# A gated recurrence on one core: the second half of each step's scans worked chunk by chunk

## The chip, the cores and the metric

The kernel runs on one core of a Trainium2 chip. A core has a matrix engine (TensorE, PE in the profile; its weight loads are shown as PEld), a vector engine (VectorE, DVE), a scalar engine for activation functions (ScalarE, ACT), a general engine (GpSimd, POOL) and a queue engine for transfers (SyncE, SP). The metric is the device time of one execution in microseconds (us). The median of three runs before the change is 1750.26 us (1750.22 to 1751.6).

## The reference

Cut to what is computed (all float32; batch 8, 512 time steps, 512 inputs and 512 state values):

```python
def step(h, x_t):
    fused = sigmoid(concatenate([x_t, h], -1) @ w_W + w_b)
    hidden_state, output_state = split(fused, 2, axis=-1)            # r, z
    memory_state = x_t @ wx_W + wx_b + hidden_state * (h @ wh_W + wh_b)
    h_new = output_state * h + (1.0 - output_state) * tanh(memory_state)
    return h_new, h_new
out = x + hs                # hs: h_new of all 512 steps
```

In the kernel's words a step is: `r` and `z` from sigmoids, `hh = h @ wh_W + wh_b`, `xx = x_t @ wx_W + wx_b`, the memory `m = r * hh + xx`, `n = tanh(m)`, and `h_new = z * h + (1 - z) * n`. The next step can't start its products before it has `h_new`.

## The kernel before

**Layout.** The 512 state values lie as four chunks of 128 on the partitions, with the batch (8) along the free dimension. Half A is chunks 0 and 1, half B is chunks 2 and 3. A group is four steps (`GS`); the step's place in its group is `s`, and `rows = slice(8 * s, 8 * s + 8)`.

**TensorE.** In each of the 512 steps (`for i in range(T)`, L208) the state is the stationary operand, 32 columns of `hT` for one chunk, and the weights `wh` stream past it. Four column groups `j` are done side by side (L221). The string `ORDER` (L25) sets the order by hand: R0 R1 G0 G1 R2 R3 G2 G3 H0 H1 H2 H3. The letter names the PSUM bank, the digit the chunk. So R<-hTA and G<-hTA (chunks 0 and 1) come first, then R<-hTB and G<-hTB (chunks 2 and 3), then H<-hTA and H<-hTB, and at the end of the step one part of the prefill `xp`, the input product for the group after the next (L223). Bank R holds the sums for `r` of both halves, G those for `hh` and `z` of half A, H those for `z` and `hh` of half B. A bank can be read once all four chunks have been added.

**From the banks to the next state.** The order of VectorE's work is written out at L294 to L303: both `turn_r`, then for half A `turn_h`, `turn_z`, `memory`, `update`, and the same four for half B. `turn_r` and `turn_z` transpose 128x64 values from PSUM to SBUF (L237), and ScalarE turns them into `r` in slot 1 of `md0` and `1 - z` in slot 2 of `hd0` (through the helper `act`, L157). `turn_h` transposes `hh` into slot 0 of `md1` (L255). `memory` runs a scan along the free dimension (L273): out = d0 * previous + d1, over pairs of slots, where a zero in slot 0 of `md0` restarts the recurrence and leaves `hh`, and slot 1 makes `r * hh + xx`. ScalarE's tanh of it goes to slot 1 of the state tile `hT`. `update` is a scan over triples of slots (L285): d0 is `hd0` with 0, -1, 1 - z in its slots, d1 is `hT` with h, n, h in its slots, so that slot 2 of the next `hT` is `(n - h) * (1 - z) + h`. ScalarE then copies the new state from slot 2 into slot 0 (L305), for the next update.

**Tiles.** `hT`, `md0`, `md1` and `hd0` of either half have the shape partition, row, chunk, slot (L109 to L116). The two chunks of a half thus alternate row by row: of one chunk, neighbouring rows of `md1` lie 16 bytes apart and those of `hT` 24.

**Around it.** After the updates, VectorE transposes a part of `xx` for the next group (`turn_x`, L187), ScalarE copies a part of the prefill into the next group's banks (`spread`, L182) or the bias into `xp` (`seed`, L165), VectorE sets `IDLE` = 5 small cells of a tile that nothing reads (L314), and POOL adds `x` to the new state into the output tile `ot`, half B first (L316). SP loads an input chunk and stores an output chunk every 16 steps. Where two instructions write and read across engines, a semaphore wait is put between them from the regions they touch. The call to `manual_schedule` (L205) leaves the order of the loop as written.

Of the kernel before, what the change touches and what calls it, by code (L numbers as in the profile page):

```python
# [7 lines left out]
F32 = mybir.dt.float32  # L8
AF = mybir.ActivationFunctionType
ALU = mybir.AluOpType  # L10
PSUM = bass.MemoryType.PSUM

P = 128
NQ = 4
GS = 4
B = 8
# [2 lines left out]


DVE_FILL = 15
IDLE = 5
SYNC = mybir.DependencyInfo(mybir.DependencyClass.Sync, mybir.DependencyReason.DATA)

ORDER = "R0 R1 G0 G1 R2 R3 G2 G3 H0 H1 H2 H3"  # L25
# [7 lines left out]
def tile_cond_rnn_residual(  # L33
# [7 lines left out]
    out: bass.AP,  # L41
    TC: int,
):

# [20 lines left out]
    nc = tc.nc  # L67
# [4 lines left out]
    const = ctx.enter_context(tc.tile_pool(name="const", bufs=1))  # L72
    xin_p = ctx.enter_context(tc.tile_pool(name="xin", bufs=4))
    out_p = ctx.enter_context(tc.tile_pool(name="outp", bufs=3))
    work = ctx.enter_context(tc.tile_pool(name="work", bufs=4))
# [4 lines left out]
    def load_x(c):  # L80
        if c < NCH:
            t_ = xin_p.tile([P, NQ, TC * B], F32, tag="xin", name=f"xin_{c}")
            nc.sync.dma_start(out=t_, in_=x[c].rearrange("p (k n) -> p k n", k=NQ))
            xins[c] = t_
# [16 lines left out]
    for k in range(NQ):  # L101
        nc.sync.dma_start(out=wh[:, k], in_=wh_d[:, k])
    load_x(1)
    load_x(2)

    NH = 2 * GS
    hT = [  # L109
        [const.tile([P, 32, 2, 3], F32, name=f"hT{n}{i}") for i in range(NH)]  # L110
        for n in "AB"
    ]

    md0 = [[const.tile([P, 32, 2, 2], F32, name=f"md0{n}{i}") for i in range(2)] for n in "AB"]
    md1 = [[const.tile([P, 32, 2, 2], F32, name=f"md1{n}{i}") for i in range(2)] for n in "AB"]
    hd0 = [[const.tile([P, B, 2, 3], F32, name=f"hd0{n}{i}") for i in range(2)] for n in "AB"]  # L116
    zeros = const.tile([P, 512], F32, name="zeros")
    nc.vector.memset(zeros, 0.0)
    for n, t_ in enumerate(hd0[0] + hd0[1] + md0[0] + md0[1] + hT[0] + hT[1]):
# [1 line left out]
    for t_ in hd0[0] + hd0[1]:  # L121
        nc.gpsimd.memset(t_[:, :, :, 1], -1.0)
    idle = const.tile([P, IDLE], F32, name="idle")

    def state(hf, i, slot=2):

        s = i % GS
        return hT[hf][i % NH][:, B * s : B * s + B, :, slot]
# [13 lines left out]
    def mm(out_, lhsT, rhs, start=False):  # L142
        nc.tensor.matmul(  # L143
            out_, lhsT, rhs, start=start, stop=False, skip_group_check=True
        )
# [10 lines left out]
    def act(key, out_, in_, func, **kw):  # L156
        inst = nc.scalar.activation(out_, in_, func, **kw).ins  # L157
        if key in written:
            tc.declare_no_dep(inst, written[key], reason="ordered through VectorE")
        written[key] = inst  # L160
        return inst

    def seed(g):

        nc.scalar.copy(xps[g % 2], bias)  # L165

    def prefill(g):

        c, t0 = divmod(g * GS, TC)
        for k in range(NQ):  # L170
            for j in range(NQ):
                mm(
                    xps[g % 2][32 * j : 32 * j + 32, 64:448],
                    xins[c][:, k, t0 * B : t0 * B + 32],
                    wx[:, k, j, :],
                )
            yield

    def spread(g, names):

        for n in names:
            nc.scalar.copy(banks[g % 2][n], xps[g % 2][:, XP[n]])  # L182

    def turn_x(g, e):

        c0 = XP["X"].start + 32 * e
        nc.vector.transpose(  # L187
            md1[e // 2][g % 2][:, :, e % 2, 1], xps[g % 2][:, c0 : c0 + 32]
        )

    def take(it, n=None):
        while n is None or n > 0:
            if next(it, it) is it:
                return
            n = None if n is None else n - 1
# [12 lines left out]
    for i in range(T):  # L208
        g, s = divmod(i, GS)
        c, t = divmod(i, TC)  # L210
        ps = banks[g % 2]
        if t == 0:
            load_x(c + 3)
            ot = out_p.tile([P, NQ, TC, B], F32, tag="ot", name=f"ot_{c}")
        if s == 0:
            pre = prefill(g + 2) if g + 2 < NG else iter(())

        for n in ORDER.split():
            bank, k = n[0], int(n[1])
            hs = hT[k // 2][i % NH][:, :, k % 2, 2]  # L220
            for j in range(NQ):  # L221
                mm(ps[bank][32 * j : 32 * j + 32, :], hs, wh[:, k, j, WH[bank]])
        take(pre, 1)  # L223

        rows = slice(B * s, B * s + B)
        def flat(t_):
            return t_.rearrange("p n c s -> p (n c s)")

        raw = {
            "h": (ps["G"][:, :HU], ps["H"][:, HU:]),  # L230
            "z": (ps["G"][:, HU:], ps["H"][:, :HU]),
            "r": (ps["R"][:, :HU], ps["R"][:, HU:]),
        }

        def turned(n, hf):
            t_ = work.tile([P, 2, 32], F32, tag=f"t{n}{hf}", name=f"t{n}{hf}_{i}")
            inst = nc.vector.transpose(t_.rearrange("p c n -> p (c n)"), raw[n][hf]).ins  # L237
            return t_[:, :, rows], inst

        r_done = [None, None]  # L240

        def turn_r(hf):
            tr, inst = turned("r", hf)

            if hf == 1 and i + 1 - NH in pool_done:
                tc.add_manual_dep(inst, pool_done[i + 1 - NH].name, SYNC)
            r_done[hf] = act(
                ("r", hf, g % 2, s),
                md0[hf][g % 2][:, rows, :, 1].rearrange("p n c -> p c n"),
                tr,  # L250
                AF.Sigmoid,
            )

        def turn_h(hf):
            nc.vector.transpose(  # L255
                md1[hf][g % 2][:, :, :, 0].rearrange("p n c -> p c n"), raw["h"][hf]
            )

        def turn_z(hf):
            tz, inst = turned("z", hf)  # L260

            tc.add_manual_dep(inst, r_done[hf].name, SYNC)
            act(
                ("zc", hf, i % 2),
                hd0[hf][i % 2][:, :, :, 2].rearrange("p n c -> p c n"),
                tz,
                AF.Sigmoid,
                scale=-1.0,
            )

        def memory(hf):
            m = work.tile([P, B, 2, 2], F32, tag=f"m{hf}", name=f"m{hf}_{i}")
            nc.vector.tensor_tensor_scan(  # L273
                flat(m),
                flat(md0[hf][g % 2][:, rows]),
                flat(md1[hf][g % 2][:, rows]),
                0.0,
                ALU.mult,
                ALU.add,
            )  # L280
            act(("n", hf, i % NH), state(hf, i, 1), m[:, :, :, 1], AF.Tanh)

        def update(hf):
            s1 = (i + 1) % GS
            nc.vector.tensor_tensor_scan(  # L285
                flat(hT[hf][(i + 1) % NH][:, B * s1 : B * s1 + B]),
                flat(hd0[hf][i % 2]),
                flat(hT[hf][i % NH][:, rows]),
                0.0,
                ALU.mult,  # L290
                ALU.add,
            )

        turn_r(0)  # L294
        turn_r(1)
        turn_h(0)
        turn_z(0)
        memory(0)
        update(0)
        turn_h(1)  # L300
        turn_z(1)
        memory(1)
        update(1)  # L303
        for hf in range(2):
            act(("h", hf, (i + 1) % NH), state(hf, i + 1, 0), state(hf, i + 1), AF.Copy)  # L305

        if g + 1 < NG:
            turn_x(g + 1, s)
            if s < 3:
                spread(g + 1, "RGH"[s])  # L310
            elif g + 3 < NG:
                seed(g + 3)
        for n in range(IDLE):
            nc.vector.memset(idle[:, n : n + 1], 0.0)  # L314
        for hf in (1, 0):
            pool_done[i + 1] = nc.gpsimd.tensor_tensor(  # L316
                ot[:, 2 * hf : 2 * hf + 2, t, :].rearrange("p c n -> p n c"),
                xins[c][:, 2 * hf : 2 * hf + 2, t * B : t * B + B].rearrange("p c n -> p n c"),
                state(hf, i + 1),
                ALU.add,  # L320
            ).ins
        if t == TC - 1:
            nc.sync.dma_start(out=out[c], in_=ot.rearrange("p k t b -> p (k t b)"))
            xins.pop(c)
# [62 lines left out]
```

## Time and profile before

| | |
|---|---|
| median of the runs | 1750.26 us |
| the profiled execution | 1748.49 us, of which the span of the trace is 1746.7 us |
| granted TensorE clock, mean | 0.998 |
| step, transpose of R to transpose of R, median | 3.36 us |
| VectorE busy | 1070.4 us, 61% of the span |
| ScalarE busy | 929.0 us, 53% |
| POOL busy | 230.9 us, 13% |
| scan m of half B (128x32), mean | 225 ns, 512 times |
| update scan of half B (128x48), mean | 258 ns, 512 times |
| tanh of half B (128x16), mean | 228 ns, 512 times |
| transposes of `hh` into md1B, mean | 282 ns, 512 times |

The first 21.7 us of the span bring in weights and make the first prefill, and from the first transpose of R on, the 512 steps follow each other at a nearly constant pace. To read it: a step is a circle through TensorE, VectorE and ScalarE, and while one engine works on one half, another can work on the other. The sum of an engine's busy time says little here. The timeline of a single step, with the idle time before each instruction and what ended it, says which handover comes last.

### The profile page before, as it was taken

Reading aid. Unit: us, or ns where it says so; the run is one execution under the profiler, and the core shown is the slowest. Engines: PE = TensorE matmul, PEld = TensorE weight load, DVE = VectorE, ACT = ScalarE, POOL = GpSimd, SP = SyncE. Lnnn points to the kernel's source line nnn. Section 1 sums busy time; section 2 is a strip of 40 time slices with the busy share of each in tenths; the row PEclk is TensorE's granted clock in tenths of the full one; section 3 lists DMA queues with packets and bytes.
Section 4 is the critical chain, followed back from the end, with each engine's and each line's share of the span. In section 5 each row is a group of like instructions: output and inputs, shape, how many; then the busy total and the mean of one; then the engine's idle time right before and its main releaser. Section 6 shows DMA issues by size and latency. Waiting matters only on the chain.

```text
span 1746.7 us, 121040 instructions
## 1 busy us (share of the span) xinstructions
PE 1732.3 (99%) x53312; PEld 1454.8 (83%) x53312; DVE 1070.4 (61%) x8212; ACT 929.0 (53%) x4610; POOL 230.9 (13%) x1041
## 2 busy tenths in 40 slices
PE   8999999999999999999999999999999999999998
PEld 5888888888888888888888888888888888888887
DVE  3666666666666666666666666666666666666665
ACT  3555555555555555555555555555555555555554
POOL 1111111111111111111111111111111111111111
PEclk9999999999999999999999999999999999999999
DMA  4000000000000000000000000000000000000000
GB/s 177 17 7 13 16 17 16 17 5 16 17 16 17 5 16 17 16 17 4 17 17 17 16 16 5 17 17 16 17 4 17 17 16 17 4 17 10 11 11 10
DMA packets 11232, 31.09 MB, mean 18 GB/s; under 512 B 1360, under 2 KB 1360, under 8 KB 10704
## 3 DMA queue, kind: packets, MB, share of 16 engines
q1 hardware_dynamic: 10368, 23.07, 3.8%
q8 instruction: 416, 6.82, 1.6%
q14 instruction: 112, 0.92, 0.2%
q10 hardware_dynamic: 336, 0.28, 0.0%
HBM read 14.96 MB, written 8.39 MB: 13 GB/s over the span
## 4 chain that ended last, share of the span: by engine, by line
PE 98%; DMA 1%; DVE 0%; issue 0%; ACT 0%; ACTq 0%; POOL 0%; POOLq 0%
PE R L143 28%; PE G L143 26%; PE H L143 25%; PE xp L143 19%; DMA wh<-in_wh_dram 1%; DMA bias<-in_bias_dram 0%; DVE md1A L255 0%; DVE hTA L285 0%; ACT hd0A L157 0%; ACT hTA L157 0%; ACTq L89 0%; POOL ot L316 0%; DVE tz L237 0%; POOLq L381 0%; DVE hTB L285 0%
## 5 line engine op out<-in xcount | busy, mean ns | idle before, releaser
L143 PE MATMUL xp<-wx,xin 128*32 128x384 f32 x4096 | 425.5, 489 | 3.9 <-ACT xp L165 3.9
L143 PEld LDWEIGHTS R<-wh,hTA 128*32 128x32 f32 x8192 | 239.1, 136 | 216.9 <-DVE hTA L285 216.4
L237 DVE STREAM_TRANSPOSE tr<-R 128x64 f32<-128x64 f32 x1024 | 194.8, 228 | 329.5 <-PE R L143 329.5
L143 PE MATMUL R<-wh,hTB 128*32 128x128 f32 x8192 | 344.2, 285 | 1.6 <-DMA wh<-in_wh_dram 1.6
L316 POOL TENSOR_TENSOR ot<-xin,hTB 128x16 f32<-128x16 f32 x512 | 126.9, 248 | 1512.1 <-DVE hTB L285 1399.4
L143 PE MATMUL R<-wh,hTA 128*32 128x128 f32 x8192 | 318.0, 273 | 2.6 <-DVE hTA L285 2.6
L143 PE MATMUL G<-wh,hTB 128*32 128x128 f32 x8192 | 317.6, 273 | 0.0
L143 PE MATMUL H<-wh,hTB 128*32 128x128 f32 x8192 | 317.6, 273 | 0.0
L143 PE MATMUL G<-wh,hTA 128*32 128x128 f32 x8192 | 317.6, 273 | 0.0
L143 PE MATMUL H<-wh,hTA 128*32 128x128 f32 x8192 | 317.6, 273 | 0.0
L157 ACT ACTIVATE hd0B<-tz 128x16 f32<-128x16 f32 x512 | 118.9, 232 | 305.4 <-DVE tz L237 305.4
L157 ACT ACTIVATE md0A<-tr 128x16 f32<-128x16 f32 x512 | 120.8, 236 | 280.3 <-DVE tr L237 280.3
L143 PEld LDWEIGHTS R<-wh,hTB 128*32 128x32 f32 x8192 | 219.6, 139 | 56.8 <-DMA wh<-in_wh_dram 1.6
L143 PEld LDWEIGHTS H<-wh,hTA 128*32 128x32 f32 x8192 | 247.7, 136 | 0.0
L143 PEld LDWEIGHTS H<-wh,hTB 128*32 128x32 f32 x8192 | 247.5, 136 | 0.0
L143 PEld LDWEIGHTS G<-wh,hTB 128*32 128x32 f32 x8192 | 247.3, 136 | 0.0
L143 PEld LDWEIGHTS G<-wh,hTA 128*32 128x32 f32 x8192 | 247.1, 136 | 0.0
L285 DVE TENSOR_TENSOR_SCAN hTB<-hd0B,hTB 128x48 f32<-128x48 f32 x512 | 132.3, 258 | 150.5 <-ACT hTB L157 149.7
L285 DVE TENSOR_TENSOR_SCAN hTA<-hd0A,hTA 128x48 f32<-128x48 f32 x512 | 132.1, 258 | 148.9 <-ACT hTA L157 148.9
L255 DVE STREAM_TRANSPOSE md1A<-G 128x64 f32<-128x64 f32 x512 | 161.0, 314 | 28.7
L157 ACT ACTIVATE hTB<-hTB 128x16 f32<-128x16 f32 x512 | 117.7, 230 | 109.9 <-DVE hTB L285 109.0
L157 ACT ACTIVATE hd0A<-tz 128x16 f32<-128x16 f32 x512 | 118.6, 232 | 102.8 <-DVE tz L237 102.8
(44 smaller groups left out, 1642.8 us busy)
## 6 DMA issues: line engine op xcount, KB each, us to landing
xin<-in_x_dram SPq DMA_DIRECT2D x32, 256.0 KB, 4.1
out_dram<-ot SPq DMA_DIRECT2D x32, 256.0 KB, 2.5
wx<-in_wx_dram SPq DMA_DIRECT2D x4, 768.0 KB, 7.2
wh<-in_wh_dram SPq DMA_DIRECT2D x4, 768.0 KB, 11.4
bias<-in_bias_dram ACTq DMA_DIRECT2D x4, 64.0 KB, 4.9
hin<-in_h_dram ACTq DMA_DIRECT2D x1, 16.0 KB, 7.7
```

Of the source, the lines that this page charges most:

```text
L143: nc.tensor.matmul(out_, lhsT, rhs, start=start, stop=False, skip_group_check=True)
L157: inst = nc.scalar.activation(out_, in_, func, **kw).ins
L237: inst = nc.vector.transpose(t_.rearrange("p c n -> p (c n)"), raw[n][hf]).ins
L255: nc.vector.transpose(md1[hf][g % 2][:, :, :, 0].rearrange("p n c -> p c n"), raw["h"][hf])
L285: nc.vector.tensor_tensor_scan(flat(hT[hf][(i + 1) % NH][:, B * s1 : B * s1 + B]), flat(hd0[hf][i % 2]), flat(hT[hf][i % NH][:, rows]), 0. ...
L316: pool_done[i + 1] = nc.gpsimd.tensor_tensor(ot[:, 2 * hf : 2 * hf + 2, t, :].rearrange("p c n -> p n c"), xins[c][:, 2 * hf : 2 * hf + 2, ...
```

## The change

In half B, the work from the scan of `r * hh + xx` on is done for one chunk at a time: two scans of 16 columns, two tanh of 8, two update scans of 24, where there was one each of 32, 16 and 48. Half A keeps its single instructions. The order on VectorE is scan of chunk 2, scan of chunk 3, update of chunk 2, update of chunk 3. So that each chunk of half B lies in one piece, its tiles now have the order partition, chunk, row, slot in memory, and are seen through a rearranged view with the old order of indices (`pair`). The work tile `m` of half B has the same new order. The products are issued in the order of before; in the built program the first matmul of R2 waits for the first update of half B, and the first matmul of R3 has a wait of its own for the second. `IDLE` goes from 5 to 3.

```diff
-IDLE = 5
+IDLE = 3
...
+    def pair(n, name, rows, slots):
+
+        if n == "A":
+            return const.tile([P, rows, 2, slots], F32, name=name)
+        return const.tile([P, 2, rows, slots], F32, name=name).rearrange("p c n s -> p n c s")
...
-    hT = [
-        [const.tile([P, 32, 2, 3], F32, name=f"hT{n}{i}") for i in range(NH)]
-        for n in "AB"
-    ]
-
-    md0 = [[const.tile([P, 32, 2, 2], F32, name=f"md0{n}{i}") for i in range(2)] for n in "AB"]
-    md1 = [[const.tile([P, 32, 2, 2], F32, name=f"md1{n}{i}") for i in range(2)] for n in "AB"]
-    hd0 = [[const.tile([P, B, 2, 3], F32, name=f"hd0{n}{i}") for i in range(2)] for n in "AB"]
+    hT = [[pair(n, f"hT{n}{i}", 32, 3) for i in range(NH)] for n in "AB"]
+
+    md0 = [[pair(n, f"md0{n}{i}", 32, 2) for i in range(2)] for n in "AB"]
+    md1 = [[pair(n, f"md1{n}{i}", 32, 2) for i in range(2)] for n in "AB"]
+    hd0 = [[pair(n, f"hd0{n}{i}", B, 3) for i in range(2)] for n in "AB"]
...
-        def flat(t_):
-            return t_.rearrange("p n c s -> p (n c s)")
+
+        def scans(hf, out_, d0, d1):
+
+            for c_ in [slice(0, 2)] if hf == 0 else [slice(0, 1), slice(1, 2)]:
+                nc.vector.tensor_tensor_scan(
+                    *[t_[:, :, c_].rearrange("p n c s -> p (n c s)") for t_ in (out_, d0, d1)],
+                    0.0,
+                    ALU.mult,
+                    ALU.add,
+                )
+                yield c_
...
         def memory(hf):
-            m = work.tile([P, B, 2, 2], F32, tag=f"m{hf}", name=f"m{hf}_{i}")
-            nc.vector.tensor_tensor_scan(
-                flat(m),
-                flat(md0[hf][g % 2][:, rows]),
-                flat(md1[hf][g % 2][:, rows]),
-                0.0,
-                ALU.mult,
-                ALU.add,
-            )
-            act(("n", hf, i % NH), state(hf, i, 1), m[:, :, :, 1], AF.Tanh)
+
+            m = work.tile([P, B, 2, 2] if hf == 0 else [P, 2, B, 2], F32, tag=f"m{hf}", name=f"m{hf}_{i}")
+            if hf == 1:
+                m = m.rearrange("p c n s -> p n c s")
+            for c_ in scans(hf, m, md0[hf][g % 2][:, rows], md1[hf][g % 2][:, rows]):
+                act(("n", hf, c_.start, i % NH), state(hf, i, 1)[:, :, c_], m[:, :, c_, 1], AF.Tanh)
 
         def update(hf):
             s1 = (i + 1) % GS
-            nc.vector.tensor_tensor_scan(
-                flat(hT[hf][(i + 1) % NH][:, B * s1 : B * s1 + B]),
-                flat(hd0[hf][i % 2]),
-                flat(hT[hf][i % NH][:, rows]),
-                0.0,
-                ALU.mult,
-                ALU.add,
-            )
+            new = hT[hf][(i + 1) % NH][:, B * s1 : B * s1 + B]
+            for _ in scans(hf, new, hd0[hf][i % 2], hT[hf][i % NH][:, rows]):
+                pass
```

## The prediction

> **What bounds the kernel now.** I read the page first: its shares of busy time and its chain name TensorE alone.
>
> ```profile
> PE 1732.3 (99%) x53312; PEld 1454.8 (83%) x53312; DVE 1070.4 (61%) x8212; ACT 929.0 (53%) x4610; POOL 230.9 (13%) x1041
> ...
> PE 98%; DMA 1%; DVE 0%; issue 0%; ACT 0%; ACTq 0%; POOL 0%; POOLq 0%
> ...
> L143 PEld LDWEIGHTS R<-wh,hTB 128*32 128x32 f32 x8192 | 219.6, 139 | 56.8 <-DMA wh<-in_wh_dram 1.6
> ```
>
> Taken at its word this leaves nothing to gain for an edit of VectorE and ScalarE. But matmul records overlap (a block is shown 0.62 us long and the next starts 0.44 later), so a late start of up to 0.18 us shows no idle PE. The weight loads do: 56.8 us idle before R<-hTB, 0.11 us for each of the 512 steps. So I went to the timeline of one step in the middle (start us, length us, engine, what, idle before and its releaser):
>
> ```profile
> 900.01 0.38 DVE L237 STREAM_TRANSPOSE tr<-R 128x64 f32<-128x64 f32 x2 [0.64 <-PE R L143]
> ...
> 901.07 0.83 PE L143 MATMUL xp<-wx,xin 128*32 128x384 f32 x8
> 901.31 0.26 DVE L285 TENSOR_TENSOR_SCAN hTA<-hd0A,hTA 128x48 f32<-128x48 f32 x1 [0.29 <-ACT hTA L157]
> 901.48 0.28 DVE L255 STREAM_TRANSPOSE md1B<-H 128x64 f32<-128x64 f32 x1
> 901.62 0.47 PEld L143 LDWEIGHTS R<-wh,hTA 128*32 128x32 f32 x16 [0.42 <-DVE hTA L285]
> 901.63 0.21 DVE L237 STREAM_TRANSPOSE tz<-H 128x64 f32<-128x64 f32 x1
> 901.71 0.62 PE L143 MATMUL R<-wh,hTA 128*32 128x128 f32 x16
> 901.80 0.23 DVE L273 TENSOR_TENSOR_SCAN m<-md0B,md1B 128x32 f32<-128x32 f32 x1
> 901.87 0.23 ACT L157 ACTIVATE hd0B<-tz 128x16 f32<-128x16 f32 x1 [0.60 <-DVE tz L237]
> 902.04 0.48 PEld L143 LDWEIGHTS G<-wh,hTA 128*32 128x32 f32 x16
> 902.06 0.23 ACT L157 ACTIVATE hTB<-m 128x16 f32<-128x16 f32 x1
> 902.15 0.62 PE L143 MATMUL G<-wh,hTA 128*32 128x128 f32 x16
> ...
> 902.32 0.26 DVE L285 TENSOR_TENSOR_SCAN hTB<-hd0B,hTB 128x48 f32<-128x48 f32 x1 [0.29 <-ACT hTB L157]
> ...
> 902.63 0.43 PEld L143 LDWEIGHTS R<-wh,hTB 128*32 128x32 f32 x16
> 902.63 0.67 PE L143 MATMUL R<-wh,hTB 128*32 128x128 f32 x16
> ...
> 903.12 0.62 PE L143 MATMUL G<-wh,hTB 128*32 128x128 f32 x16
> ...
> 903.37 0.38 DVE L237 STREAM_TRANSPOSE tr<-R 128x64 f32<-128x64 f32 x2 [0.64 <-PE R L143]
> ```
>
> One step is 903.37 - 900.01 = 3.36 us. The circle: the update of half B ends (902.32 + 0.26 = 902.58), the weight loads of R<-hTB start 0.05 later (902.63), the R bank is complete, the first transposes start at 903.37, and the chain of transposes, scans and tanh comes round to the update again. The load of G<-hTA began at 902.04; blocks of this size follow each other 0.437 us apart, so R<-hTB could have begun loading at 902.48, and it began at 902.63. Its matmuls are shown from 902.63, at the same time as their load; elsewhere matmuls trail their load by 0.11. In the records the second group of four starts 0.16 us after the first instead of 0.11, so the block really starts at about 902.63 + 0.053 = 902.68. It was due 0.437 after G<-hTA: 902.15 + 0.437 = 902.585.
>
> **So TensorE loses about 0.097 us a step.** Cross-check by its own pace: six blocks of 0.437 and the prefill xp (901.07 to 901.71) make 2.62 + 0.645 = 3.265; 3.362 (the median step) less 3.265 is 0.097. 511 such steps are 49.6 us, the most that the change can bring. That a step follows the end of B's update one to one has a witness: in the second step of the run that update ended 2.642 us after the step's first transpose instead of 2.569, and the step took 3.434 instead of 3.362. Half A is not on the circle: its load waits until 901.62 for hTA, but its matmuls at 901.71 come exactly 0.645 after xp, with some 0.04 to spare.
>
> **The change, part by part.** I count in ns from a step's first tr transpose (medians over the steps of this trace: md1B transposed from 1476 to 1758, tz from 1623, scan m of B 1792 to 2016, tanh 2050, update 2311 to 2569, R<-hTB load 2622).
>
> The scan m of B becomes two of 16 columns. The rows: 225 ns for 32 columns, 258 for 48, so 2.06 a column; 16 columns come to 192. Chunk 0 is then ready 33 earlier.
>
> The tanh of 8 columns: no such row. 228 at 16 columns is the upper end; the 128x128 copies take some 260, so width costs little; lower end 220. I take 226.
>
> The update becomes two of 24 columns: 258 - 24 x 2.06 = 209. That is 49 earlier.
>
> With the waits kept (34 from scan to tanh, 33 from tanh to update, 53 from update to load) chunk 0 is ready 33 + 2 + 49 = 84 earlier from these alone.
>
> The transpose md1B<-H writes a step of 8 bytes where it wrote one of 16 (the chunks now lie one behind the other). Its row today: 282; the transpose tz from the same bank, written densely: 207. The scan starts 34 after this transpose, so it may gain. The Trainium skill ("SBUF — State Buffer", on cachelines) says lines are 16 bytes, that a walk which touches each line twice is free and one that takes a new line at every access pays. By it the transpose falls to 207. That the strided row is dearer than the dense one fits, but no row has a step of 8 bytes. By the rule the scan would start when tz lets go of VectorE, near 1765 (a dense transpose passes on after about 140 to 150), 27 earlier; by the present row 0 earlier. I take the middle, 13, and keep both ends.
>
> Sum: chunk 0 is ready 84 to 111 earlier, 97 in the middle. TensorE can use only 97. By the lower end a step becomes 3.278, by the middle and upper 3.265. I take 94 a step, a little under the cap because the middle just reaches it: 511 x 0.094 = **48 us**.
>
> Chunk 1 is what was added, and must not take this back. R's blocks on hTB are issued chunk 0 (8 matmuls, 218 ns), then chunk 1; in the built program the first matmul of each has a wait of its own, for the first and the second update. VectorE passes on from a scan before its recorded end (hTA at 901.31, next start 901.48: 175 after a start of 258), 83 early; so the second scan starts near 192 - 83 = 109 after the first. ScalarE takes activations 130 apart (md0A to md0B), so the second tanh is 130 behind, and the second update too: chunk 1 ends near 2472 + 130 = 2602. It is needed at its load, some 218 after a chunk 0 load due at 2525, less the 53: 2690. It has 88 to spare. Here a rule speaks against the change: the Trainium skill ("VectorE: DVE Perf Modes", the drain that can't be avoided) has the next operation not begin until the pipe is empty, so that pieces pay what one tile pays once. By rule: second scan from the end of the first, its tanh at about 2195, second update from 2472 to 2681: 9 to spare, still no loss. The row decides; the sum is the same by either.
>
> Nothing else reaches the circle. The second scan, tanh and update lie in idle time: VectorE waits 0.64 us for R before each step, ScalarE 0.55 (280.3 us in 512 waits before md0A), and the copies hTA and hTB to slot 0, moved by at most 130, are needed only at the next step's updates. Were that cover gone, each would cost its passing time, 109 to 130. Two memsets less give some 10 to 20 ns in the same idle time: nothing; VectorE's program keeps 16 instructions a step, ScalarE's goes from 9 to 10. POOL waits for B's second update (perhaps 35 later) and has 2.9 of 3.4 us idle; behind it only the store at a chunk's end waits, 0.03 us at the very end. No DMA is added or moved.
>
> The profiled execution took 1748.49 (span 1746.7, 1.8 around it): 1748.5 - 48 = 1700.5. The median of the runs is 1750.26, 1.8 above it, so **1702.3**.
>
> **Rivals.**
> 1. Partial gain: narrow instructions have a floor (the 128x16 copies of hin took 175, so a scan of 16 may not fall to 192), or the second wait inside the block costs PE a part of the 53. For it: no row shows such a scan. Against: the slope from 48 to 32 columns is clean. Half the gain, 45 to 50 ns a step: about 1726.
> 2. No change: a scan costs 225 and 258 whatever its width, and the transpose stays. Then chunk 0 is as late as before: 1750.
> 3. Slower: the second chunk decides, on PE, in R<-hTB. It begins to cost when chunk 1 ends after 2690, and past 2690 + 97 = 2787 the kernel is slower than before. With both updates gating the block's start, as if PE couldn't begin on chunk 0 alone, the load would come at 2602 + 53 = 2655 instead of 2622: +33 ns a step, +17 us, 1767. For it: each step gets one more handover on three engines. Against: the separate waits in the program, and 88 ns to spare.
> That the change doesn't do what it says is this third case.
>
> **How the numbers follow.** Forecast (saving 80 to 99 a step) 0.78, rival 1 0.10, rival 2 0.03, rival 3 0.09. A difference of 0.2%, 3.5 us, is what a measurement can tell from none. The forecast's own bounds are 511 x 82 = 42 us (no gain in the transpose, tanh at 228) and 49.6 us, so 1700.7 to 1708.4; with a few us for the pace of PE, which nobody has seen without the stall, and a part of rival 1: 1697 to 1715. Faster 0.88 (forecast and rival 1), same 0.03, slower 0.09.
>
> **What would show it.** Right: a step near 3.27; the load of R<-hTB at most 0.45 after G<-hTA's, its idle of 56.8 us mostly gone; scans of 128x16 near 192 and 128x24 near 209; md1B's transpose between 207 and 282; the idle of R<-hTA's load as today, 0.42. Wrong: idle of R<-hTB's load in the middle of its block (rival 3), a 16-column scan above 215 (rivals 1 and 2), or steps at 3.27 bounded by hTA, whose slack is only 0.04.

## The result, and the profile after

The changed kernel takes 1699.40 us (median of four runs, 1698.07 to 1700.3) against 1750.49 us before (four runs as well, 1750.22 to 1751.6; three of them gave the 1750.26 above): 51.1 us less, a ratio of 0.9706 with a 95% interval of 0.969 to 0.9723. The profiled execution took 1700.3 us, its span is 1698.5.

From the page after the change, the engines' busy time, the shares of the chain, and the weight loads of R<-hTB:

```profile
PE 1684.0 (99%) x53312; PEld 1474.7 (87%) x53312; DVE 1084.3 (64%) x8212; ACT 923.6 (54%) x5122; POOL 232.4 (14%) x1041
...
PE 98%; DMA 1%; DVE 0%; issue 0%; ACT 0%; ACTq 0%; POOL 0%; POOLq 0%
...
L147 PEld LDWEIGHTS R<-wh,hTB 128*32 128x32 f32 x8192 | 250.0, 122 | 2.9 <-DMA wh<-in_wh_dram 1.6
```

PE stands at 99% and the chain at 98%, exactly as before, although the kernel lost 48 us of span. These two rows can't tell a stalled TensorE from a full one. The third can: the idle time before R<-hTB's weight loads fell from 56.8 us to 2.9, and what is left lies in the first 30 us of the run.

One step of the changed kernel in the timeline (columns as before the change):

```profile
899.32 0.38 DVE L250 STREAM_TRANSPOSE tr<-R 128x64 f32<-128x64 f32 x2 [0.61 <-PE R L147]
...
900.93 0.49 PEld L147 LDWEIGHTS R<-wh,hTA 128*32 128x32 f32 x16 [0.39 <-DVE hTA L234]
...
900.99 0.68 PE L147 MATMUL R<-wh,hTA 128*32 128x128 f32 x16
901.07 0.26 DVE L234 TENSOR_TENSOR_SCAN m<-md0B,md1B 128x16 f32<-128x16 f32 x2
901.18 0.23 ACT L161 ACTIVATE hd0B<-tz 128x16 f32<-128x16 f32 x1 [0.60 <-DVE tz L250]
901.30 0.30 ACT L161 ACTIVATE hTB<-m 128x8 f32<-128x8 f32 x2
...
901.53 0.31 DVE L234 TENSOR_TENSOR_SCAN hTB<-hd0B,hTB 128x24 f32<-128x24 f32 x2 [0.20 <-ACT hTB L161]
...
901.79 0.49 PEld L147 LDWEIGHTS R<-wh,hTB 128*32 128x32 f32 x16
901.86 0.68 PE L147 MATMUL R<-wh,hTB 128*32 128x128 f32 x16
...
902.58 0.38 DVE L250 STREAM_TRANSPOSE tr<-R 128x64 f32<-128x64 f32 x2 [0.59 <-PE R L147]
```

The step is 902.58 - 899.32 = 3.26 us; the median over steps 40 to 499 is 3.265, and nearly every one of them lies within 1 ns of it, while those of before scattered over 20 ns or so. The load of R<-hTB now leads its matmuls by 0.07 instead of sharing their start. It still begins only when chunk 0 is ready, 53 ns after the first update's end, but that is early enough: the matmuls follow those of G<-hTA at TensorE's own pace (901.43 to 901.86; 0.437 in the median). The row of 0.31 us with x2 holds both updates.

In the tables below all places are ns from a step's first transpose of R, medians over steps 40 to 499.

| half B | before | after |
|---|---|---|
| transpose md1B<-H | 1476 to 1757 | 1471 to 1699 |
| scan of m | 1791 to 2016 | 1750 to 1924, 1841 to 2009 |
| tanh | 2050 to 2278 | 1981 to 2179, 2081 to 2279 |
| update | 2311 to 2569 | 2211 to 2420, 2336 to 2520 |
| load R<-hTB starts | 2622 | 2473 |
| step | 3362 | 3265 |

### The profile page after: what moved, and what is told of

Same layout as the page of the kernel before. It is cut to its first block, busy times and chain, and to the rows that moved or that the text cites. A ratio compares the mean times of both kernels' runs of the same rounds, so it can differ in the third digit from the quotient of the medians.

```text
span 1698.5 us, 121555 instructions
## 1 busy us (share of the span) xinstructions
PE 1684.0 (99%) x53312; PEld 1474.7 (87%) x53312; DVE 1084.3 (64%) x8212; ACT 923.6 (54%) x5122; POOL 232.4 (14%) x1041
## 4 chain that ended last, share of the span: by engine, by line
PE 98%; DMA 1%; DVE 0%; issue 0%; ACT 0%; ACTq 0%; POOL 0%; POOLq 0%
PE R L147 26%; PE G L147 26%; PE H L147 26%; PE xp L147 19%; DMA wh<-in_wh_dram 1%; DMA bias<-in_bias_dram 0%; DVE md1A L268 0%; DVE hTA L234 0%; ACT hd0A L161 0%; ACT hTA L161 0%; ACTq L90 0%; DVE tz L250 0%; POOL ot L320 0%; DVE hTB L234 0%; POOLq L385 0%
## 5 line engine op out<-in xcount | busy, mean ns | idle before, releaser
L147 PE MATMUL xp<-wx,xin 128*32 128x384 f32 x4096 | 449.6, 488 | 3.1 <-ACT xp L169 3.1
L147 PE MATMUL R<-wh,hTA 128*32 128x128 f32 x8192 | 343.3, 273 | 2.7 <-DVE hTA L234 2.5
L147 PE MATMUL H<-wh,hTA 128*32 128x128 f32 x8192 | 343.0, 273 | 0.0
L147 PE MATMUL G<-wh,hTB 128*32 128x128 f32 x8192 | 342.9, 273 | 0.0
L147 PE MATMUL H<-wh,hTB 128*32 128x128 f32 x8192 | 342.8, 273 | 0.0
L147 PE MATMUL G<-wh,hTA 128*32 128x128 f32 x8192 | 342.4, 273 | 0.0
L147 PEld LDWEIGHTS H<-wh,hTA 128*32 128x32 f32 x8192 | 272.0, 136 | 0.1
L147 PEld LDWEIGHTS G<-wh,hTA 128*32 128x32 f32 x8192 | 271.6, 136 | 0.0
L147 PEld LDWEIGHTS R<-wh,hTB 128*32 128x32 f32 x8192 | 250.0, 122 | 2.9 <-DMA wh<-in_wh_dram 1.6
L234 DVE TENSOR_TENSOR_SCAN hTB<-hd0B,hTB 128x24 f32<-128x24 f32 x1024 | 157.7, 196 | 104.1 <-ACT hTB L161 104.1
```

The lines of the kernel that those rows point to most:

```text
L147: nc.tensor.matmul(out_, lhsT, rhs, start=start, stop=False, skip_group_check=True)
L234: nc.vector.tensor_tensor_scan(*[t_[:, :, c_].rearrange("p n c s -> p (n c s)") for t_ in (out_, d0, d1)], 0.0, ALU.mult, ALU.add,)
```

## The experiments

The theory on trial is the prediction's: a step follows the end of the update that lets R<-hTB begin, one to one, until TensorE's own pace of 3.265 us takes over. Its rivals: the gain comes from something else in the change, which are cheaper weight loads (the denser state cut those of hTB from 136 to 122 ns each) or the memsets; or the whole update counts and not its first chunk. Each ratio below is to the kernel before, timed again beside the run (medians of 1751.2 to 1752.7 us).

**1. Both chunks gate the block.** The first matmul of R2 waits for the second update too (`both[i]` is the last update of half B that makes step i's state).

```diff
+                if n == "R2" and j == 0 and i in both:
+                    tc.add_manual_dep(inst, both[i].name, SYNC)
```

> The changed kernel, but the first matmul of R2 waits for both updates of half B; nothing else differs. Theory (TensorE's start on chunk 0 sets the step): the second update ends 2520 ns after the step's first transpose in the changed kernel, so the load starts at 2573 and the block at 2626, 48 after it is due; step 3.313 us, about 1724 us. Rival (the gain comes from cheaper weight loads of the denser state, 136 to 122 ns, or from fewer memsets): stays near 1699 us, since both remain.

1720.20 us, ratio 0.9818 (0.9803 to 0.9833). The lines of one step:

```profile
902.43 0.31 DVE L237 TENSOR_TENSOR_SCAN hTB<-hd0B,hTB 128x24 f32<-128x24 f32 x2 [0.20 <-ACT hTB L161]
...
902.79 0.41 PEld L147 LDWEIGHTS R<-wh,hTB 128*32 128x32 f32 x16
902.79 0.66 PE L147 MATMUL R<-wh,hTB 128*32 128x128 f32 x16
```

Load and matmuls start together again, the mark of a late state. The updates lie where they lay in the changed kernel (the second ends at 2520), the load starts at 2574 instead of 2473, and the step is 3.302 us. About 20 of the 51 us thus come from TensorE being allowed to begin on chunk 0 alone; the cheaper loads and the fewer memsets are in this run as well.

**2. The update alone is split.** md0, md1 and m keep the old layout, their scan and the tanh stay whole.

```diff
-    md0 = [[pair(n, f"md0{n}{i}", 32, 2) for i in range(2)] for n in "AB"]
-    md1 = [[pair(n, f"md1{n}{i}", 32, 2) for i in range(2)] for n in "AB"]
+    md0 = [[pair("A", f"md0{n}{i}", 32, 2) for i in range(2)] for n in "AB"]
+    md1 = [[pair("A", f"md1{n}{i}", 32, 2) for i in range(2)] for n in "AB"]
...
-            for c_ in [slice(0, 2)] if hf == 0 else [slice(0, 1), slice(1, 2)]:
+            for c_ in [slice(0, 1), slice(1, 2)] if hf == 1 and split else [slice(0, 2)]:
```

> Half B's update alone is split in two, with the new layout of hT and hd0; scan of m, tanh, md0 and md1 are as before the change. Theory: the tanh ends as before (2278), the first update starts at 2311 and takes 208, ends 2519, load 2572, 47 late; step 3.312 us, about 1723 us, half of the gain. Rival (denser state, cheaper loads): the state is dense here too, so about 1699 us.

1720.26 us, ratio 0.9822 (0.9806 to 0.9838). The first update ends at 2525, the load starts at 2578, the step is 3.307 us. More than half of the gain (32 of 51 us) comes from this part: 55 ns a step, of which 44 are the earlier update and 11 the cheaper loads, as the table further down shows.

**3. Scan and tanh alone are split.** hT and hd0 keep the old layout, and the update is whole.

```diff
-    hT = [[pair(n, f"hT{n}{i}", 32, 3) for i in range(NH)] for n in "AB"]
+    hT = [[pair("A", f"hT{n}{i}", 32, 3) for i in range(NH)] for n in "AB"]
...
-    hd0 = [[pair(n, f"hd0{n}{i}", B, 3) for i in range(2)] for n in "AB"]
+    hd0 = [[pair("A", f"hd0{n}{i}", B, 3) for i in range(2)] for n in "AB"]
```

> Scan of m and tanh of half B are split in two, with the new layout of md0 and md1; the update is one instruction of 48 columns over the old layout of hT and hd0. Theory: the update must wait for the second tanh, which ends at about 2303 where the single one ended at 2278; update 2336 to 2594, load 2647, 122 late; step 3.387 us, about 1762 us, slower than before. Rival (the earlier scan and tanh bring the gain by themselves): 1700 to 1725 us. Rival (denser state): 1750 us, for the state is as before.

1755.03 us against 1752.04, ratio 1.0016 (1.0007 to 1.0025): a little slower than before, as expected, by less than expected. In its timeline

```profile
902.84 0.30 ACT L161 ACTIVATE hTB<-m 128x8 f32<-128x8 f32 x2
...
903.17 0.26 DVE L234 TENSOR_TENSOR_SCAN hTB<-hd0B,hTB 128x48 f32<-128x48 f32 x1 [0.30 <-ACT hTB L161]
...
903.48 0.43 PEld L147 LDWEIGHTS R<-wh,hTB 128*32 128x32 f32 x16
```

the whole update waits for the second tanh, which ends at 2288 where the single one ended at 2278. The second scan ends at 2013, hardly before the single one (2016), and its tanh stands behind the first on ScalarE until 2085. All that scan, tanh and layout had won for chunk 0 is lost in that one wait. I had put the update at 2336, where the changed kernel's second update stands behind the first; alone it starts at 2320, and the step of the trace is 3.372 us, 10 ns over before (the 3 us between the medians are 6 ns a step).

**4 and 5. Chunk 0 held back.** A memset of a tile that nothing reads stands in front of the two updates, of 512 or 400 columns.

```diff
+            if hf == 1:
+                nc.vector.memset(fill, 0.0)
             for _ in scans(hf, new, hd0[hf][i % 2], hT[hf][i % NH][:, rows]):
```

> The changed kernel with one memset of 512 columns of a tile that nothing reads on VectorE in front of the two updates of half B. Theory: it holds the first update from 2211 to about 2353 ns, so that it ends at 2561, load 2614, 89 late; step 3.354 us, about 1745 us: nearly the whole gain is gone though every part of the change is in place. Rival (cheaper loads, fewer busy engines): VectorE idles 0.59 us in a step, the memset takes 0.49, so 1699 us.

> As the run with 512 columns in front of the updates, but with 400. The first update is held to about 2259 ns and ends at 2467 or a little before, 48 later than in the changed kernel. Theory with the threshold of the prediction (2472): no loss, 1699 to 1701 us. Theory with the slack read from the changed kernel's trace, where the fourth column group runs 60 ns behind and the block starts 31 earlier against the transposes (threshold 2440): 27 ns a step lost, about 1713 us. Rival (cheaper loads): 1699 us.

1764.89 us (ratio 1.0076, 1.0061 to 1.0091) and 1705.22 us (0.9733, 0.9719 to 0.9748). One step with 512 columns:

```profile
901.16 0.48 DVE L297 MEMSET fill<- 128x512 f32 x1
...
901.56 0.24 DVE L235 TENSOR_TENSOR_SCAN hTB<-hd0B,hTB 128x24 f32<-128x24 f32 x2
...
901.76 0.41 PEld L148 LDWEIGHTS R<-wh,hTB 128*32 128x32 f32 x16
901.76 0.66 PE L148 MATMUL R<-wh,hTB 128*32 128x128 f32 x16
```

Every part of the change is in place here, the cheaper loads and the fewer `IDLE` memsets too, and the whole gain is gone. The time is 20 us above what I expected, because the memset held the first update longer than counted, to 2466 and not to 2353 (the last section has a memset's cost). So chunk 0 ends at 2610, and the step is 3.392 us. With 400 columns it ends at 2493 and the step is 3.276. This table shows what the two delays and the other edits did to the step:

| kernel | load R<-hTB starts | step | difference |
|---|---|---|---|
| before | 2622 | 3362 | 740 |
| scan and tanh split (hT as before) | 2631 | 3372 | 741 |
| chunk 0 held, 512 columns | 2663 | 3392 | 729 |
| update split | 2578 | 3307 | 729 |
| both chunks gate | 2574 | 3302 | 728 |
| chunk 0 held, 400 columns | 2547 | 3276 | 729 |
| changed kernel | 2473 | 3265 | TensorE's pace |

From load to the next step it is always 740 or 741 with the old layout of the state and 728 or 729 with the dense one. The 11 to 12 ns between them are what the cheaper weight loads are worth, and only where the block is late. It fits the first load of a late block, which no running block covers: that load fell from 133 to 122 ns. The rival was right that they are cheaper, and wrong in its size. With 729, the load is due at 3265 - 729 = 2536, chunk 0 thus at 2483, 53 earlier. The run with 400 columns ended 10 past this and lost 11 a step. The prediction's own threshold, 2472, lacks the 11 of the cheaper loads. The tighter one of 2440, which I had read from the changed kernel's trace, would have cost 53 a step and is refuted.

**6 and 7. Chunk 1 held back**, by a memset of 160 or 320 columns between the updates.

```diff
+                if hf == 1 and _.start == 0:
+                    nc.vector.memset(fill, 0.0)
```

> The changed kernel with a memset of 160 columns between the two updates of half B. The second update is held to about 2469 ns and ends at 2653 instead of 2520; chunk 0 is untouched. Theory: the second chunk is needed at 2690, or 2659 by the changed kernel's trace, so no loss: 1699 to 1701 us. Rival (the end of the whole update counts): 133 later, 1760 us or more.

> As the run with 160 columns between the updates, but with 320. The second update is held to about 2603 ns and ends at 2787. Theory: this is 97 past the point where chunk 1 is needed (2690), the number from which the prediction held the change to be slower than before; step 3.362 us, about 1749 us. Were only chunk 0 to count: 1699 us.

1699.57 us (0.9701, 0.9685 to 0.9717), no loss, with the second update ending at 2660 instead of 2520; and 1760.39 us (1.0046, 1.0031 to 1.0061). In the timeline of the second the block of R<-hTB is cut in two:

```profile
901.52 0.21 DVE L235 TENSOR_TENSOR_SCAN hTB<-hd0B,hTB 128x24 f32<-128x24 f32 x1 [0.20 <-ACT hTB L162]
901.75 0.33 DVE L298 MEMSET fill<- 128x320 f32 x1
901.79 0.25 PEld L148 LDWEIGHTS R<-wh,hTB 128*32 128x32 f32 x8
...
901.99 0.14 DVE L235 TENSOR_TENSOR_SCAN hTB<-hd0B,hTB 128x24 f32<-128x24 f32 x1
...
902.19 0.19 PEld L148 LDWEIGHTS R<-wh,hTB 128*32 128x32 f32 x8 [0.15 <-DVE hTB L235]
```

Eight loads go at once, eight wait for the second update. It ends at 2822, its loads start at 2876, and the step is 3.384 us, 119 over TensorE's pace: chunk 1 is due at 2876 - 119 - 53 = 2704. The changed kernel has it at 2520. That a step follows chunk 1 one to one is taken over from chunk 0 here; the run with 160 columns agrees with it (2660, no loss). The memset again cost more than counted (the second update came at 2678, expected at 2603), hence 1760 instead of 1749.

**8 and 9. The memsets.** `IDLE = 5` in the changed kernel, and `IDLE = 3` alone in the kernel before.

```diff
-IDLE = 3
+IDLE = 5
```

> The changed kernel with IDLE = 5, so 18 VectorE instructions a step instead of 16. Theory: the memsets lie in VectorE's idle time before the transposes of R, no effect: 1699 us within 0.2%. Rival (the number of memsets or of VectorE's instructions a step matters): several us slower.

> The kernel before the change with IDLE = 3 alone. Theory: no effect, 1750 us within 0.2%. Rival (the memsets matter): faster by some us.

1698.99 us (0.9697, 0.9683 to 0.9712) and 1750.80 us (1.0, 0.999 to 1.001). The memsets and the number of VectorE's instructions in a step (18 and 14 here) do nothing to the time that these runs could tell.

**10. Half A split as well**, to see whether TensorE really is the limit that is left, or the circle through half A, whose load of R<-hTA has little room. Half A's tiles get the new layout too, and `IDLE` is 1.

```diff
-            for c_ in [slice(0, 2)] if hf == 0 else [slice(0, 1), slice(1, 2)]:
+            for c_ in [slice(0, 1), slice(1, 2)]:
```

> The changed kernel with half A split in the same way and IDLE = 1 (VectorE again has 16 instructions a step). Theory: the changed kernel's steps are set by TensorE's own pace of 3.265 us, so 504 of the 511 steps can't become shorter; only the last seven, which have no prefill and take 3.220, may, by at most 0.1 us each: 1698 to 1700 us. Rival (the circle through half A, whose load has 13 ns to spare, still sets the step): A's update comes some 80 ns earlier and the time falls by 10 us or more.

1698.38 us (0.97, 0.9685 to 0.9714), 1 us from the changed kernel and not to be told from it. The load of R<-hTA moved from 1607 to 1465, and the step stayed at 3.265. Only the last steps, which have no prefill, went from 3.220 to 3.160 us. So half A is not the limit, and handing over earlier on both halves doesn't shorten the other steps. Less work on TensorE might; it wasn't tried.

## Why the prediction was right

**The loss on TensorE and its cap: right to the ns.** The forecast read 0.097 us a step out of starts that no idle time of PE shows, and a pace of 3.265. The changed kernel's step is 3.265, and experiment 10 shows that earlier handovers bring it no lower. The slope of one, for which the prediction had a single late step as its witness, is now shown by six kernels.

**Chunk 0: mechanism right, sizes too small.** It was put 84 to 111 earlier, 97 in the middle; it came 149 earlier (2569 to 2420). Term by term: the scan of 16 columns was to save 33, it saved 51 (174 ns, expected 192); the transpose md1B was to bring the scan forward by 13, at most 27, it brought 41 (the scan now starts 131 after the transpose tz, where 140 to 150 were counted, and not 34 after md1B's end); the tanh was to save 2, it saved 30 (198, expected 226 and at least 220); the update was to save 49, it saved 49 (209). Left out was a queue: ScalarE takes the tanh of chunk 0 only 122 ns after its sigmoid into hd0B (1859 to 1981; 122 or 123 in every run with the split scan), although the scan ended at 1924 and 34 more would have done. That took back 23. The sum is 51 + 41 + 30 + 49 - 23 = 148. As TensorE could use only some 86 of it (2569 to 2483), none of these errors reached the time; the step came to rest on the cap, which the forecast took to be just reached. That the sizes didn't matter is the cap's doing, not theirs. The other 11 of the 97 came from the cheaper loads of the denser state, which the forecast left out.

**The two rules that were weighed.** Of the cachelines in the Trainium skill ("SBUF — State Buffer", Specifications), by which a walk that meets each 16-byte line twice pays nothing, the direction holds: md1B's transpose fell from 282 to 226 ns when its step went from 16 to 8 bytes. It didn't reach the 207 of a dense one, so the step of 8 bytes, two to a line, isn't free here. Of the drain in the skill's "VectorE: DVE Perf Modes" ("The DRAIN you can't avoid") the row was rightly preferred: the second scan starts 91 ns after the first, which lasts 174. The section itself leaves room for this: "A next op that is not held starts earlier". The late starts of the memsets in experiments 4 to 7 look like a witness for the rule and are none: they depend on the memset's width, as the last section shows, and the update behind each memset starts 82 to 84 ns before the memset's end.

**Chunk 1: right, with more room than stated.** Put at 2602 and due at 2690, it ends at 2520 and is due at 2704. The slower rival could have come true: past 2704 + 97 = 2801 the kernel would lose against before, and the run with 320 columns, at 2822, did. The changed kernel is far from it.

**Marks.** Idle of R<-hTB's loads: mostly gone, as said. Idle of R<-hTA's: 0.39, said 0.42. The mark "at most 0.45 after G<-hTA's" was missed (2003 to 2473, 0.47): R<-hTB's load still waits for chunk 0 (2420 + 53 = 2473) and comes 33 after TensorE's pace. The mark was drawn at the load; what counts is the matmuls, and these are on time (2110 to 2547, 0.437).

**The time.** In the profiled executions 48.2 us were gained (1748.49 to 1700.3), 48 were forecast. That they agree so closely is luck: a step gained 97 ns and not the 94 of the forecast, which makes 1.5 us, and a few odd steps in the trace of the changed kernel took about as much back (one lasted 3.81 us, the very first 4.32 where it was 3.56 before). Medians moved by 51.1, a little over the 49.6 that was to be had (the interval goes from 48 to 54), and the forecast of 1702.3 was 2.9 too high. The term that failed is the last one: I added the 1.8 us between the median and the profiled execution of before, but the profiled execution of the changed kernel was the slowest of its four runs. The distance between one execution and the median isn't a constant of the kernel.

## What to carry to other kernels

When an engine is shown 99% busy by overlapping records, compare the start-to-start distance of its blocks with what it keeps where nothing is late; here the difference was what a faster handover could bring, and no more. To split the last stretch of a chain helps only if the consumer begins on the first piece: splitting the stages ahead of a whole update made the kernel a little slower, splitting the update alone (with its denser state) brought more than half, and both together brought all that the consumer could use. When a piece is added behind another, work out by when it is needed, and check the queue of every engine that it passes, not only of the one that is split.

## What was unexpected in the hardware

- The same scan of 24 columns is recorded as 208 ns after idle time, 184 behind another scan and 144 behind a memset. A duration from a row holds for the place in which it was taken.
- A memset's row understates what the memset adds to VectorE's chain. Its start is recorded later the wider it is: against the end of the instruction ahead, 18 ns before it with 160 columns, and 16, 32 and 55 after it with 320, 400 and 512. Its end lies 174, 341, 424 and 540 after that same end, 1.04 ns a column, while the recorded durations (192, 325, 392, 485) grow by 0.83. The kernel's own memsets of 192 columns, one behind another at the start of the run, fit in (11 before, 207 after). Scans and transposes start some 80 ns before the end of the one ahead. The expectations for experiments 4 to 7, which left this out, put the updates behind the memsets 47 to 113 ns too early.
- The four column groups of TensorE can run apart at the same pace of 0.437 us a block. In the trace of the changed kernel, the first group leads the others by 28 ns up to the step of 3.81 us (blocks of 0.65 us), and from there until the prefills end the fourth trails by some 60 (blocks of 0.68). In the kernel before, where a block is late in every step, they lie in line (0.62).
- Halving the step between the state's values (24 to 12 bytes) took each of half B's weight loads from 136 to 122 ns, and half A's as well in experiment 10.
